# Attention and mixture of experts: the causal mask moves from TensorE products to GpSimd selects

## The chip, the cores and the metric

The kernel runs on one core of one Trainium2 chip. The metric is the device time of one execution in microseconds (us). The engines are named as in the profile: PE (TensorE, matrix products), PEld (its weight loads), ACT (ScalarE), DVE (VectorE), POOL or Pool (GpSimd) and SP (SyncE, which issues most DMAs).

## The reference

For x of 8 batch rows x 1024 positions x 512 features (f32), the reference computes

```python
x = x + attn(layernorm(x))      # 16 heads of 32 features
x = x + moe(layernorm(x))       # 8 experts, the best 2 per token, capacity 160 per batch row
```

In the attention, Q and K of a head are the cosines and sines (from an interpolated table) of angles that depend on x and on the position, 64 features each; V is the sum of such a cosine and sine. What matters here:

```python
scores = jnp.einsum('bqhd,bkhd->bhqk', Q, K) / scale
causal = jnp.triu(jnp.ones((S, S), dtype=bool), k=1)
scores = jnp.where(causal, -jnp.inf, scores)
attn = jax.nn.softmax(scores, axis=-1)
```

The experts' part picks two experts per token, gives each token a slot of its expert (at most 160 per batch row and expert; the rest is dropped), runs two matrix layers with relu, and adds the gated rows back.

## The kernel before

**Steps.** The attention runs in 32 steps `n`; step n works on batch row b = n // 4 and a group c = n % 4 of four heads, which are two pairs of heads. For each pair, and for each half h of the queries (512 of 1024), `scores` makes tiles of scores with the keys on the 128 partitions and the queries along the row, for both heads of the pair at once: 128 x 2 x 512 in two PSUM banks. A half h has 4h full tiles with earlier keys and then four blocks of keys of its own half, which are cut by the diagonal: the first block has 512 queries, the second 384, the third 256, the fourth 128. `tiles_of` puts the second and the fourth into one tile, so a half has 4h + 3 tiles, and three of them need the mask, with four diagonal blocks of 128 x 128 in all.

**Scores, weights, sums.** The products of K and Q (line L679) use 64 rows of PE each, so the two heads of a pair run side by side. ACT takes the exponential of a tile from PSUM to a tile `e` in SBUF (L699); it subtracts no maximum. `attend` then multiplies `e` with V (L713); a column of V that holds a constant makes the sum of the weights, by which `turn` divides later (transposes L215 into PSUM, reciprocal L748, product L750).

**The mask before.** Behind the score products of a tile with own keys, PE adds a large negative number to the scores of later keys: `keys_b` (rows of an identity, bf16) times `later_b` (0 or -FAR, bf16), in two parts of 64 keys for each of the two heads, that is four small products per tile (L693). The exponential makes zeros of these. `rest_of_loads` and `mask` prepare `keys_b` and `later_b` on Pool at the start.

**The order of the work.** PE, ACT, DVE and SP run in the order in which the program is written (`manual_schedule`); Pool's order is a planner's, except where `keep_in_program_order` holds an instruction in the written order. The written order interleaves generators: `some(5, *ahead)` makes the next five score tiles, `some(3, *products)` the next three tiles of `attend`. A plain step has four bursts of score tiles:

1. all three tiles of the first pair's half 0 and two of its half 1; then the last four tiles of the previous step's last `attend`,
2. the other five tiles of half 1; then `turn` of the previous step, and all of `attend` for the first pair (3 + 7 tiles),
3. for the second pair two tiles of half 0, `turn` of the first pair, the third tile, two tiles of half 1; in three of four steps the transposes for the step after next; then `attend` for half 0 (3 tiles),
4. the other five tiles of half 1; then, in the next step, `attend` for half 1.

The score tiles, the transposes of `turn`, those of Q and K and the router's products share three PSUM buffers of two banks (`two_banks`).

**Angles.** For the next steps DVE makes the angles of Q and K from transposed x (L520, into `qk_f`), shifts them (L440, `angle`, into `qk_r`), ACT squares (L444, `square`), takes absolute values (L580) and sines (L589, L447), and DVE multiplies (L450, `times`) into `qk_c` and `qk_r`; SP's DMAs carry these into the layout of the score products (L604). `qk_r` and `qk_c` have one buffer each. V's angles go through L621, L626 and L440, the output's through L642, L440, L450 and L653. ACT loads a table between sines and exponentials, twice a step.

**Router and scatters.** In the steps of batch row b the router of row b - 1 runs in pieces (`router`; layer norm L807, products L869 and L852, choice of experts L876 to L968). It ends in step c = 3 with a list `scatters` of 16 entries, one for each 128 tokens and choice: an indirect DMA on Pool that writes token numbers and gates to the experts' slots in DRAM (L764). Each waits for the landing of the one before, since they write one tensor. `scatter()` issues all 16 at that place, for rows 0 to 5; for the last two rows they are issued in `ending`, half of row 6's first. `fetch_slots` (L991) brings the finished slots of a row into SBUF two batch rows later in the program; the planner places it.

**The experts** follow the attention (L1175 and L1220, a Strassen-like scheme). Weight mixtures of the first of them run on Pool (L1159), in written order.

The parts of `scores` that the change touches, in the program's own words:

```python
own_keys = parts[0][0] >= 4 * h
...
        nc.tensor.matmul(
            out_, lhsT=keys_b[r, part, :], rhs=late,
            start=False, stop=part == 1, skip_group_check=True,
        )
e = ep.tile([P, 2, n], F32, name=f"e_{n}", bufs=8 if n == 512 else 2)
```

Of the kernel before, what the change touches and what calls it, by code (L numbers as in the profile page):

```python
# [11 lines left out]
F32 = mybir.dt.float32  # L12
I32 = mybir.dt.int32
U16 = mybir.dt.uint16
BF16 = mybir.dt.bfloat16
AF = mybir.ActivationFunctionType
ALU = mybir.AluOpType
# [4 lines left out]
P = 128  # L22
B, S, D = 8, 1024, 512
H, DH = 16, 32
NT = B * S
NTT = S // P
NCH = D // P
# [28 lines left out]
UNIT = COS_HALF / LIFT  # L56
# [7 lines left out]

FIRST = 6 * P
REACH = [(0, -(-FIRST // CAP)), (FIRST // CAP, B)]

FAR = 1000.0 * math.sqrt(2 * DH) / (UNIT * UNIT)

ROOT_GUESS = float(0x5F3759DF)  # L70

# [2 lines left out]
def preln_attn_moe_kernel(  # L74
# [21 lines left out]
    nc = tc.nc  # L96
# [35 lines left out]
    own = to_router.pool("own", 1, **left)  # L132
# [3 lines left out]
    row2 = to_router.pool("row2", 2, **left)  # L136
# [44 lines left out]
    ident = const.tile([P, P], F32, name="ident")  # L181
# [4 lines left out]
    for t in (base_first, room[0]):  # L186
        nc.gpsimd.iota(
            t, pattern=[[0, 2], [1, S]], base=0, channel_multiplier=0,
# [19 lines left out]
    def two_banks():  # L208
        return ps_sc.tile([P, 2, 512], F32, name="ps_s")
# [21 lines left out]
    def first_stats(t0, t1):  # L231
        for t in range(t0, t1):
            st = small.tile([P, nc.vector.BN_STATS_DIM], F32, name="st")
            nc.vector.bn_stats(st, first_tiles[t])
            nc.vector.bn_aggr(first_mv[:, t, :], st)
# [14 lines left out]
    ps = two_banks()[:, 0, : 6 * NCH]  # L250
# [8 lines left out]
    nc.gpsimd.memset(ones, 1.0)  # L259

    before = own.tile([P, P], F32, name="before")


    keys_b = own.tile([P, 2, P], BF16, name="keys_b")
    nc.gpsimd.memset(keys_b, 0.0)
    later_b = own.tile([P, 2, P], BF16, name="later_b")
    e_row = own.tile([P, E], F32, name="e_row")
    e_row_low = own.tile([P, E], F32, name="e_row_low")
    dropped = own.tile([P, NTT, TOPK], F32, name="dropped")
# [12 lines left out]
    empty = own.tile([P, E * CAP // P, 2], I32, name="empty")  # L282
    nc.vector.memset(empty, 0)

    later = row2.tile([P, NCH, 2 * P], F32, name="xT", bufs=1)[:, :3, :P]

    def mask():
        for part in range(2):
            for a in range(2):
                r = slice(a * 64, (a + 1) * 64)  # L290
                nc.gpsimd.tensor_copy(later_b[r, part, :], later[r, 1 + part - a, :])
                nc.gpsimd.tensor_copy(keys_b[r, part, part * 64 : part * 64 + 64], ident[r, r])

    def rest_of_loads():

        nc.gpsimd.memset(later, 0.0)
        for i in range(3):
            nc.gpsimd.affine_select(
                out=later[:, i, :], in_=later[:, i, :], compare_op=ALU.is_ge, fill=-FAR,
                base=64 * (1 - i), pattern=[[1, P]], channel_multiplier=-1,  # L300
            )
        nc.gpsimd.affine_select(
            out=before, in_=ones, compare_op=ALU.is_gt, fill=0.0, base=0, pattern=[[1, P]],
            channel_multiplier=-1,
        )
        nc.gpsimd.iota(
            e_row, pattern=[[1, E]], base=0, channel_multiplier=0,
            allow_small_or_imprecise_dtypes=True,
        )
        nc.gpsimd.iota(  # L310
            e_row_low, pattern=[[1, E]], base=-E, channel_multiplier=0,
            allow_small_or_imprecise_dtypes=True,
        )
        nc.gpsimd.iota(
            dropped, pattern=[[P * TOPK, NTT], [1, TOPK]], base=E * CAP,
            channel_multiplier=TOPK, allow_small_or_imprecise_dtypes=True,
        )
        nc.gpsimd.iota(
            empty[:, :, 0], pattern=[[0, E * CAP // P]], base=NT, channel_multiplier=1
        )  # L320
        for a in range(2):
            nc.sync.dma_start(
                inv_o[a * 64 : a * 64 + DH, :],
                w_out.rearrange("(q a d) -> a d q", a=2, d=DH)[a],
            )
        nc.sync.dma_start(wr_sb[:, :, :E], Wr.rearrange("(c p) e -> p c e", p=P))
        nc.vector.tensor_reduce(
            gather_e, ident.rearrange("p (c k) -> p k c", k=32)[:, :E, :], AX.X, ALU.add
        )
        nc.sync.dma_start(br_b, br.partition_broadcast(P))  # L330
        for i in range(NCH):
            nc.sync.dma_start(out[NT:, i * P : (i + 1) * P], zero)
            for t in xn2_d:
                nc.sync.dma_start(t[t.shape[0] - P :, i * P : (i + 1) * P], zero)
        for b in range(B):
            nc.sync.dma_start(
                slot_d[b][: E * CAP, :].rearrange("(p j) c -> p (j c)", p=P),
                empty.rearrange("p j c -> p (j c)"),
            )
# [319 lines left out]
    def tiles_of(h):  # L659


        def block(kb, at=0):
            q0 = max(512 * h, kb * P)
            return kb, q0, 512 * (h + 1) - q0, at

        d = 4 * h
        full = [[block(kb)] for kb in range(d + 1)]
        return full + [[block(d + 1), block(d + 3, 3 * P)], [block(d + 2)]]

    def scores(pair, h, es):  # L670

        for parts in tiles_of(h):
            n = sum(w for _, _, w, _ in parts)
            ps = two_banks()
            own_keys = parts[0][0] >= 4 * h
            for kb, q0, w, at in parts:
                for a in range(2):
                    r = slice(a * 64, (a + 1) * 64)
                    nc.tensor.matmul(  # L679
                        ps[:, a, at : at + w], lhsT=pair[r, 1, kb * P : (kb + 1) * P],  # L680
                        rhs=pair[r, 0, q0 : q0 + w], start=at == 0, stop=not own_keys,
                        skip_group_check=True,
                    )
            if own_keys:

                for part, w in ((0, 64), (1, P)):
                    for a in range(2):
                        r = slice(a * 64, (a + 1) * 64)
                        out_, late = ps[:, a, :w], later_b[r, part, :w]
                        if len(parts) == 2:  # L690
                            out_ = ps[:, a, :].rearrange("p (k q) -> p k q", q=P)[:, ::3, :w]
                            late = late.unsqueeze(1).to_broadcast([64, 2, w])
                        nc.tensor.matmul(  # L693
                            out_, lhsT=keys_b[r, part, :], rhs=late,
                            start=False, stop=part == 1, skip_group_check=True,
                        )

            e = ep.tile([P, 2, n], F32, name=f"e_{n}", bufs=8 if n == 512 else 2)
            nc.scalar.activation(  # L699
                e, ps[:, :, :n], AF.Exp, scale=UNIT * UNIT / math.sqrt(2 * DH)  # L700
            )
            es.append(e)
            yield

# [48 lines left out]
        )  # L753


    scatters = []
    scattered = {b: [] for b in range(B)}
    mixed = []

    def scatter(count=2 * NTT * TOPK, together=False):  # L760

        for _ in range(min(count, len(scatters))):
            b, idx, src = scatters.pop(0)
            queued = nc.gpsimd.indirect_dma_start(  # L764
                out=slot_d[b], out_offset=bass.IndirectOffsetOnAxis(ap=idx, axis=0),
                in_=src, in_offset=None,
            )
            ins = queued.ins
            if together:
                tc.add_manual_dep(  # L770
                    ins, mixed[-1].name,
                    mybir.DependencyInfo(
                        mybir.DependencyClass.NoSync, mybir.DependencyReason.DATA
                    ),
                    reason="behind the mixture",
                )
                for other in scattered[b]:
                    tc.declare_no_dep(ins, other, reason="rows of their own")
            scattered[b].append(ins)

    def router(b):
# [556 lines left out]
    next(base0)  # L1338
    next(base1)
    rest_of_loads()  # L1340
    mask()
    first_stats(2, NTT)
    layernorm_first()
    rest(base0)
# [12 lines left out]
    for n in range(NCK):  # L1357
        more, late = n + 1 < NCK, last is not None
        b, c = divmod(n, NCH)
# [87 lines left out]
        if c == 3 and b > 0:  # L1447
            next(route)
            if b > 1:
                fetch_slots(b - 2)  # L1450
            if b < B - 1:
                scatter()


        some(3, *products)
# [61 lines left out]
    def ending():  # L1517

        o_st = o_pre(NCK - 1, pos_n)
        scatter(NTT * TOPK // 2, together=True)  # L1520
        yield
        sine(o_st[1])
        square(o_st[0])
        for _ in range(3):
            yield
        for _ in o_post(NCK - 1, o_st):
            yield
        yield
        for name in router(B - 1):
            if name == "tiles":  # L1530
                scatter(together=True)

            for _ in range({"tiles": 5, "places": 5}.get(name, 1)):
                yield
        fetch_slots(B - 2)
        scatter(together=True)
        fetch_slots(B - 1)
# [33 lines left out]
```

## Time and profile before

| what | value |
|---|---|
| time, median of 3 runs | 3274.41 us (3272.74 to 3276.23) |
| time of the profiled execution | 3277.64 us |
| its span, first to last instruction | 3275.9 us |
| mean granted clock of PE | 0.996 |
| busy PE / DVE / ACT / POOL, share of the span | 97% / 69% / 40% / 13% |
| mask products L693 | 1536, first at 36.4 us, last at 1274.1 us |
| exponentials L699 | 640, mean 938 ns |
| scatters L764 | 128, mean 1268 ns |

Times in the views are microseconds from the first instruction unless marked ns. A line of a timeline gives start, duration, engine, line of the kernel, operation, output and inputs by the program's names, shapes, and the number of instructions merged; in brackets the idle time of the engine just before, and what ended it. A line of the waits gives who waited for whom, the sum in us, how many times, and the longest. A line of the stretches gives a window, its length, and the busy time and number of instructions of each engine. Ends of matmuls are modelled by the profiler, so starts are the safer figures.

### The profile page before, as it was taken

What the parts mean: (1) busy time and instruction counts of PE and PEld (TensorE: products, weight loads), DVE (VectorE), ACT (ScalarE), POOL (GpSimd) and SP (SyncE); (2) the same over time, 40 slices, a digit from 0 to 9 for tenths busy, and PEclk for the clock granted to TensorE, in tenths of its full rate; (3) what the DMA queues carried; (4) which work ended last, traced back from release to release, by engine and by line L of the source; (5) the groups of instructions that cost most, each with busy time, mean ns of one, the idle gap of its engine ahead of it and who ended that gap; (6) DMA issues with size and microseconds to landing.
All of it is one profiled execution on the core that took longest, in us unless ns stands there. A gap on an engine that the chain in (4) does not pass through costs nothing.

```text
span 3275.9 us, 48751 instructions
## 1 busy us (share of the span) xinstructions
PE 3190.8 (97%) x18942; PEld 2164.6 (66%) x18942; DVE 2255.8 (69%) x4961; ACT 1323.3 (40%) x1617; POOL 426.2 (13%) x387
## 2 busy tenths in 40 slices
PE   5999999999999999999999999999999999999998
PEld 2444444444444444588688688688688688688687
DVE  8887888878788675755755855855855855855854
ACT  7888887878787874201201201201201201201201
POOL 3000202011110213311011011011011011011010
PEclk9999999999999999999999999999999999999999
DMA  5435454453645352322322322322322322322321
GB/s 162 143 97 166 133 147 139 132 155 104 181 114 158 91 162 70 114 54 73 103 46 73 103 46 73 103 47 72 103 48 71 104 48 69 106 49 69 105 42 26
DMA packets 235254, 319.74 MB, mean 98 GB/s; under 512 B 22456, under 2 KB 155280, under 8 KB 222992
## 3 DMA queue, kind: packets, MB, share of 16 engines
q1 hardware_dynamic: 211664, 273.38, 28.6%
q0 software_dynamic: 22912, 43.22, 7.4%
q8 instruction: 150, 2.46, 0.3%
q14 instruction: 80, 0.66, 0.1%
q10 hardware_dynamic: 448, 0.02, 0.0%
HBM read 187.62 MB, written 61.82 MB: 76 GB/s over the span
## 4 chain that ended last, share of the span: by engine, by line
PE 57%; DVE 0%; DMA 0%; issue 0%; POOLq 0%; POOL 0%; DVEq 0%
PE ps_p L1220 29%; PE ps_p L1175 27%; PE ps_t L1121 1%; DMA slots<-slot_d 0%; DMA out_dram<-y,slots 0%; DVE w L1053 0%; DVE w_t L1054 0%; DVE w_t L1052 0%; DVE w_t L1055 0%; POOLq L1567 0%; POOL slot_d L764 0%; POOL slots L991 0%; DVE y L1236 0%; DVE p L1257 0%; DVE p L1258 0%
## 5 line engine op out<-in xcount | busy, mean ns | idle before, releaser
L699 ACT ACTIVATE e<-ps_s 128x1024 f32<-128x1024 f32 (+1 forms) x640 | 569.7, 938 | 202.5 <-PE ps_s L679 113.6
L679 PE MATMUL ps_s<-qk 64*128 64x512 f32 (+3 forms) x3072 | 601.9, 507 | 40.3 <-DMA qk<-qk_r 12.4
L1220 PE MATMUL ps_p<-w,hid 128*128 128x256 f32 x2560 | 567.1, 379 | 0.0
L1220 PEld LDWEIGHTS ps_p<-w,hid 128*128 128x128 f32 x2560 | 484.0, 190 | 66.6 <-DVE hid L1193 0.5
L713 PE MATMUL av<-e,v 128*64 128x512 f32 (+3 forms) x3072 | 524.7, 491 | 0.0
L1220 PE MATMUL ps_p<-w_t,hid 128*128 128x256 f32 x1920 | 430.5, 379 | 2.0 <-DVE w_t L1054 2.0
L679 PEld LDWEIGHTS ps_s<-qk 64*128 64x128 f32 x3072 | 262.0, 188 | 231.4 <-issue 111.7
L1220 PEld LDWEIGHTS ps_p<-w_t,hid 128*128 128x128 f32 x1920 | 361.1, 190 | 50.1 <-DVE w_t L1054 2.8
L713 PEld LDWEIGHTS av<-e,v 128*64 128x64 f32 x3072 | 200.8, 137 | 284.7 <-issue 268.1
L1175 PE MATMUL ps_p<-xe,w 128*128 128x256 f32 (+1 forms) x1024 | 297.8, 434 | 0.0
L1175 PE MATMUL ps_p<-xe_s,t 128*128 128x256 f32 (+1 forms) x1024 | 296.9, 433 | 0.0
L1175 PE MATMUL ps_p<-xe,t 128*128 128x256 f32 (+1 forms) x1024 | 296.8, 433 | 0.0
L764 POOL DMA_INDIRECT slot_d<-token,slot x128 | 162.4, 1268 | 974.3 <-issue 627.4
L1251 ACT COPY p<-ps_p 128x256 f32<-128x256 f32 x40 | 14.7, 369 | 604.3 <-PE ps_p L1220 604.3
L1175 PEld LDWEIGHTS ps_p<-xe,t 128*128 128x128 f32 x1024 | 194.4, 190 | 80.9 <-issue 0.4
L1175 PEld LDWEIGHTS ps_p<-xe_s,t 128*128 128x128 f32 x1024 | 194.3, 190 | 80.7 <-issue 0.4
L1175 PEld LDWEIGHTS ps_p<-xe,w 128*128 128x128 f32 x1024 | 193.4, 190 | 80.8 <-DVE hid L1193 3.5
L1080 POOL DMA_INDIRECT xg<-xn_d,source x76 | 75.2, 990 | 1074.8 <-PE ps_t L1121 1064.0
L1242 POOL DMA_INDIRECT out_dram<-y,slots x80 | 126.5, 1582 | 624.1 <-DVE y L1237 624.1
L1190 ACT ACTIVATE p<-ps_p,b_t 128x256 f32<-128x256 f32 (+1 forms) x128 | 65.5, 511 | 336.2 <-PE ps_p L1175 182.1
L1207 ACT ACTIVATE hid<-hid,b_more 128x256 f32<-128x256 f32 (+1 forms) x128 | 71.8, 561 | 274.8 <-DVE hid L1206 270.0
L1194 ACT ACTIVATE hid<-hid 128x256 f32<-128x256 f32 (+1 forms) x128 | 60.1, 470 | 299.5 <-DVE hid L1193 295.3
(224 smaller groups left out, 3818.6 us busy)
## 6 DMA issues: line engine op xcount, KB each, us to landing
w<-in_L_ffn_W_dram SPq DMA_DIRECT2D x256, 256.0 KB
w<-in_L_ffn_W_dram SPq DMA_DIRECT2D x64, 512.0 KB
qk<-qk_c SPq DMA_DIRECT2D x124, 256.0 KB
qk<-qk_r SPq DMA_DIRECT2D x124, 256.0 KB
qk_base<-base_d SPq DMA_DIRECT2D x28, 1024.0 KB
xn_d<-xn SPq DMA_DIRECT2D x72, 256.0 KB
x_mid<-in_L_attn_x_dram SPq DMA_DIRECT2D x16, 1024.0 KB
out_dram<-x_mid SPq DMA_DIRECT2D x8, 2048.0 KB
```

Of the source, the lines that this page charges most:

```text
L679: nc.tensor.matmul(ps[:, a, at : at + w], lhsT=pair[r, 1, kb * P : (kb + 1) * P], rhs=pair[r, 0, q0 : q0 + w], start=at == 0, stop=not own ...
L699: nc.scalar.activation(e, ps[:, :, :n], AF.Exp, scale=UNIT * UNIT / math.sqrt(2 * DH))
L713: nc.tensor.matmul(av[a * 64 : (a + 1) * 64, q0 - 512 * h :], lhsT=vt[:, kb, 2 * pr + a, :], rhs=es[i][:, a, at : at + w], start=kb == 0, ...
L764: queued = nc.gpsimd.indirect_dma_start(out=slot_d[b], out_offset=bass.IndirectOffsetOnAxis(ap=idx, axis=0), in_=src, in_offset=None,)
L1080: ins = nc.gpsimd.indirect_dma_start(out=xg, out_offset=None, in_=xn2_d[i % 2], in_offset=bass.IndirectOffsetOnAxis(ap=source[:, e, j0 + j ...
L1121: nc.tensor.transpose(ps[:, c, :], xg[:, c * P : (c + 1) * P], ident)
L1175: nc.tensor.matmul(ps, lhsT=weights[:, k, :], rhs=rows[:, k, :], start=k == 0, stop=k == 1)
L1190: nc.scalar.activation(p1, product(b11, a11), AF.Identity, bias=b1_t[:, e * NHC + q : e * NHC + q + 1])
L1194: nc.scalar.activation(h11, h11, AF.Relu)
L1207: nc.scalar.activation(h12, h12, AF.Relu, bias=more)
L1220: nc.tensor.matmul(ps, lhsT=hs[k][:, part, cols], rhs=ws[k][weight], start=k == 0, stop=k == NHQ - 1,)
L1242: ins = nc.gpsimd.indirect_dma_start(out=out, out_offset=bass.IndirectOffsetOnAxis(ap=meta[:, e, jj[r], 0:1], axis=0), in_=ys[r], in_offse ...
```

## The change

The bf16 products and what they are made from are gone. Instead, behind the exponential of a tile with own keys, Pool sets the weights of later keys to zero in place, one instruction for each diagonal block (128 keys x 2 heads x 128 queries). These instructions keep the written order. Scatters are issued two at a time behind the last tile of each half's scores, also in written order, rather than all 16 at one place; `hold` keeps row 6's back for `ending`, as before.

```diff
-FAR = 1000.0 * math.sqrt(2 * DH) / (UNIT * UNIT)
...
-    keys_b = own.tile([P, 2, P], BF16, name="keys_b")
-    nc.gpsimd.memset(keys_b, 0.0)
-    later_b = own.tile([P, 2, P], BF16, name="later_b")
...
-    later = row2.tile([P, NCH, 2 * P], F32, name="xT", bufs=1)[:, :3, :P]
-
-    def mask():
...
-        nc.gpsimd.memset(later, 0.0)
-        for i in range(3):
-            nc.gpsimd.affine_select(
...
     def scores(pair, h, es):
-        for parts in tiles_of(h):
+        tiles = tiles_of(h)
+        for parts in tiles:
...
-                        rhs=pair[r, 0, q0 : q0 + w], start=at == 0, stop=not own_keys,
+                        rhs=pair[r, 0, q0 : q0 + w], start=at == 0, stop=True,
...
-            if own_keys:
-
-                for part, w in ((0, 64), (1, P)):
-                    for a in range(2):
-                        r = slice(a * 64, (a + 1) * 64)
-                        out_, late = ps[:, a, :w], later_b[r, part, :w]
-                        if len(parts) == 2:
...
-                        nc.tensor.matmul(
-                            out_, lhsT=keys_b[r, part, :], rhs=late,
-                            start=False, stop=part == 1, skip_group_check=True,
-                        )
 
             e = ep.tile([P, 2, n], F32, name=f"e_{n}", bufs=8 if n == 512 else 2)
             nc.scalar.activation(
                 e, ps[:, :, :n], AF.Exp, scale=UNIT * UNIT / math.sqrt(2 * DH)
             )
+            if own_keys:
+
+                for _, _, _, at in parts:
+                    own_ = e[:, :, at : at + P]
+                    tc.keep_in_program_order(
+                        nc.gpsimd.affine_select(
+                            out=own_, in_=own_, compare_op=ALU.is_ge, fill=0.0, base=0,
+                            pattern=[[0, 2], [1, P]], channel_multiplier=-1,
+                        )
+                    )
+            if parts is tiles[-1] and not hold[0]:
+
+                scatter(2)
             es.append(e)
...
-    scatters = []
+    scatters, hold = [], [False]
...
     def scatter(count=2 * NTT * TOPK, together=False):
...
+            else:
+                tc.keep_in_program_order(queued)
...
     rest_of_loads()
-    mask()
...
-            if b < B - 1:
-                scatter()
+            hold[0] = b == B - 1
```

More of the change, by code (lines that the diff above doesn't have):

```diff
@@ L283, in preln_attn_moe_kernel @@
     nc.vector.memset(empty, 0)
-    later = row2.tile([P, NCH, 2 * P], F32, name="xT", bufs=1)[:, :3, :P]
-    def mask():
-        for part in range(2):
-            for a in range(2):
-                r = slice(a * 64, (a + 1) * 64)
-                nc.gpsimd.tensor_copy(later_b[r, part, :], later[r, 1 + part - a, :])
-                nc.gpsimd.tensor_copy(keys_b[r, part, part * 64 : part * 64 + 64], ident[r, r])
-    def rest_of_loads():
-        nc.gpsimd.memset(later, 0.0)
-        for i in range(3):
-            nc.gpsimd.affine_select(
-                out=later[:, i, :], in_=later[:, i, :], compare_op=ALU.is_ge, fill=-FAR,
-                base=64 * (1 - i), pattern=[[1, P]], channel_multiplier=-1,
-            )
+    def rest_of_loads():
         nc.gpsimd.affine_select(
@@ L680, in scores @@
                         ps[:, a, at : at + w], lhsT=pair[r, 1, kb * P : (kb + 1) * P],
-                        rhs=pair[r, 0, q0 : q0 + w], start=at == 0, stop=not own_keys,
+                        rhs=pair[r, 0, q0 : q0 + w], start=at == 0, stop=True,
                         skip_group_check=True,
                     )
-            if own_keys:
-                for part, w in ((0, 64), (1, P)):
-                    for a in range(2):
-                        r = slice(a * 64, (a + 1) * 64)
-                        out_, late = ps[:, a, :w], later_b[r, part, :w]
-                        if len(parts) == 2:
-                            out_ = ps[:, a, :].rearrange("p (k q) -> p k q", q=P)[:, ::3, :w]
-                            late = late.unsqueeze(1).to_broadcast([64, 2, w])
-                        nc.tensor.matmul(
-                            out_, lhsT=keys_b[r, part, :], rhs=late,
-                            start=False, stop=part == 1, skip_group_check=True,
-                        )
             e = ep.tile([P, 2, n], F32, name=f"e_{n}", bufs=8 if n == 512 else 2)
```

## The prediction

> **What bounds the kernel.** I read the stretches first, then the waits, then the timelines of one step. The attention stage runs to about 1275 us in 32 steps (one batch row and one group of four heads each). Busy time of three successive steps:
>
> ```profile
> core 0: us, PE busy (x) PEld busy (x) DVE busy (x) ACT busy (x) POOL busy (x), PEclk, DMA share, GB/s
> ...
> 845.00:884.00 39.00, 35.74 (x372) 18.66 (x366) 26.06 (x40) 28.36 (x28) 3.67 (x5) 0.96 0.77 230
> 884.00:922.60 38.60, 38.55 (x330) 18.57 (x326) 31.39 (x70) 33.72 (x36) 0.00 (x0) 1.00 0.51 147
> 922.60:961.00 38.40, 38.35 (x314) 19.18 (x314) 32.45 (x68) 34.00 (x35) 5.93 (x4) 1.00 0.51 142
> ```
>
> PE is busy all through a plain step, but ACT (34.0 of 38.4) and DVE (32.5) have only 4.4 and 5.9 us to spare. The first row holds a router's work, and there PE itself has 3.3 us of idle time. After 1290 us PE works on the experts without a gap; the change leaves that part alone. The waits of 60 to 1230 us show a second loop:
>
> ```profile
> DVE qk_r L440 <- DMA qk<-qk_r: 45.9, 23, 3.3
> ...
> ACT qk_f L444 <- DVE qk_r L440: 9.9, 16, 1.6
> ...
> PE ps_s L679 <- DVE prob L876: 9.0, 11, 2.2
> ```
>
> DVE's rotation (L440) waits for the landing of the previous rotation's DMA in 23 steps, ACT's squares (L444) wait for L440 in 16, and the next exponentials come behind the squares on ACT. Once a batch PE waits for the router's DVE chain.
>
> **What is removed.** One score burst on PE:
>
> ```profile
> 923.62 0.25 PE L693 MATMUL ps_s<-later_b,keys_b 64*128 64x64 bf16 x4
> 923.71 1.09 PE L679 MATMUL ps_s<-qk 64*128 64x384 f32 x8
> 924.63 0.33 PE L693 MATMUL ps_s<-later_b,keys_b 64*128 64x128 bf16 x4
> 924.79 0.60 PE L679 MATMUL ps_s<-qk 64*128 64x256 f32 x4
> 925.23 0.25 PE L693 MATMUL ps_s<-later_b,keys_b 64*128 64x64 bf16 x4
> 925.31 1.95 PE L679 MATMUL ps_s<-qk 64*128 64x512 f32 x8
> ```
>
> Matmul ends are modelled, so I take start to start: 0.09 + 0.16 + 0.08 = 0.33 us for twelve mask products. There are 1536, so 128 such sets: 42 us of PE, 1.33 per step. That is the ceiling of the gain.
>
> Not all of it arrives. The step has four bursts of five score tiles, and three PSUM buffers. In the first, ACT runs the five exponentials without a gap (923.97, 4.47 us), and the fifth tile (starting near 926.23) needs the buffer of the second exponential (ending near 926.08): PE comes earlier, but keeps only about 0.1 us. In the second burst the transposes (934.73) need the third exponential (end near 934.45): about 0.2 more is kept. In the third, ACT comes from a table load:
>
> ```profile
> 943.01 1.28 ACT L699 ACT_TABLE_LOAD   x1
> 944.47 2.75 ACT L699 ACTIVATE e<-ps_s 128x1024 f32<-128x1024 f32 x3 [0.17 <-PE ps_s L693]
> ```
>
> It is free at 944.29 and waited 0.17 us for a mask: again 0.15. Only the fourth burst, where ACT waits 2.50 us for PE, keeps the whole 0.33. So PE's own loop gives 0.1 + 0.2 + 0.15 + 0.33 = 0.78 us per step. The second loop gives less: exponentials of burst one, transposes of burst two, scores and transposes of burst three, L450 on qk_r (946.95 to 949.23), its DMA, L440 at 956.75 (after 2.3 us of waiting for the landing), squares, next exponentials at 960.10. Masks ahead of its PE parts were worth about 0.2 in burst two and 0.09 + 0.16 in burst three: 0.45 us per step. The slower loop decides; with the 0.1 to 0.3 us that it still has in hand, 0.5. In the seven steps with a router DVE works from 829.4 to 844.6 us with hardly a gap, and PE stands 2.2 us for L876 at 855.4: I give these nothing. Gain: 25 x 0.5 = 12.5 us (bounds 0 and 42).
>
> The mask's preparation (memsets, three affine selects, eight casts, under 4 us on Pool before 17.4 us) goes too. Pool then idles 13.7 us until L566 at 31.4, waiting for DVE: worth nothing. Were that cover gone, 4 us.
>
> **What is added.** Per set four affine selects in place (one, two, one), 512 in all, 128 partitions x 256 elements. Nearest row: L298, 128x128, 284 ns, starts 0.25 apart. A memset grows from 195 ns (128 columns) to 410 (384), so I take 0.4 us (0.25 to 0.5): 205 us of Pool, or 6.4 us per step, beside 162 us of scatters. Pool has room.
>
> Who waits for a select? The second matmul (L713) now waits for Pool where it waited for ACT. In the step shown, burst one's masked exponentials end by 926.6 and are used at 935.3; burst two's end by 936.0 and are used near 941; burst four's by 957.1, used after the next step's burst one. Burst three is the tight one: ended at 945.5, 946.6 and 947.2, used from 949.04: 3.5 us. In a batch's first step no transposes lie between (822.7 to 830.1), the cover is about 3.1 us, and L450 at 827.19 (2.28 us, two SBUF inputs) can hold the last select up: 0.2 us in 8 steps, 1.6 in all (0 to 8).
>
> The large unknown is DVE beside Pool. Pool's scatters wait for such DVE work (one at 940.72 takes 3.00 us instead of 0.96: L450 ran from 940.52 to 942.80), and DVE's median times beside scatters do not change. But beside Pool arithmetic that reads SBUF they do:
>
> ```profile
> 1331.23 0.72 POOL L1159 TENSOR_TENSOR t<-w,t 128x256 f32<-128x256 f32 x1
> 1331.91 0.73 POOL L1159 TENSOR_TENSOR t<-w 128x256 f32<-128x256 f32 x1
> ```
>
> ```profile
> 1331.26 0.22 DVE L927 TENSOR_REDUCE gate<-prob 128x8 f32<-128x64 f32 x1
> 1331.52 0.51 DVE L928 TENSOR_TENSOR tmp<-prob,gate 128x64 f32<-128x64 f32 x1
> 1332.07 0.65 DVE L929 SCALAR_TENSOR_TENSOR tmp<-tmp,e_row 128x64 f32<-128x64 f32 x1
> 1332.75 0.22 DVE L930 TENSOR_REDUCE exp_id<-tmp 128x8 f32<-128x64 f32 x1
> ```
>
> L928 and L929 take 0.23 us alone; the reductions, with one input, keep their 0.22. With L920 (0.72) and L932 (0.40) four instructions lose 1.36 us beside four Pool instructions of 0.73: 47% of Pool's time. L807, a one-input form, goes from 0.54 to 1.03 beside the same line at 1317.7. A 0.4 us select would so cost 0.19 us where DVE does nothing but such forms. Forms with two SBUF inputs (L450, L621, L626, L642, L653), and with one like L807 (L440, L414), are about 15 of the 38.4 us of a step, 40%: 0.075. A select held by one of them starts exactly at its end, in front of the next, so I take 0.1 us (0 to 0.19): 1.6 us of DVE per step.
>
> The Trainium skill, "SBUF — State Buffer", section "Who interferes with whom", speaks against this change: of VectorE (with two SBUF inputs or in a two-port mode) and GpSimd, whichever starts first holds the shared ports for its whole instruction, and the other stands. By that rule a collision can cost a whole select: at most 0.4 x 40% x 16 = 2.6 us of a router step and 0.8 of another, and the sum below would end at about +27 us rather than +10.
>
> Where it lands: in the seven router steps DVE is the bound, 7 x 1.6 = 11 us. In the other 25 most of it goes into DVE's idle 5.9 us. But L450 on qk_r follows 0.4 us after the end of an exponential whose two selects come then, and L440 (956.75) lies just behind the one that ends at 956.49: half a select each, 0.4 us per step on the second loop, 10 us (0 to 20).
>
> **Scatters.** Sixteen per batch remain, now in pairs at the end of each half's scores, in queue with the selects. The second of a pair waits for the landing of the first (236.4 us over 89 waits, at most 6.3), and the next selects stand behind it. Between burst two's last select (near 936.5) and burst three's first use (949.0) there are 12.4 us; a pair takes 0.96 + 2.7 + 0.96 typically: nothing. The two fetches of slots (L991) behind the last pair add a landing of at most 6.2 and 1.6 us, once a batch: 0 (0 to 10 in all). In the first step the position rows of L463 waited on Pool until 51.22 for a DMA; selects queued behind that would hold PE about 6 us, once: 0 (0 to 6). At the end the second weight mixture (1236 before) now comes after the last select (1275) but is used after 1290: nothing; the eight scatters behind it follow and still end before the next mixture at 1289.
>
> **Sum.** -12.5 + 1.6 + 11 + 10 = +10 us on the profiled execution's 3277.6 (span 3275.9). The median of three runs is 3.2 us below that, 3274.4; moved by 10 it is 3284.
>
> **Rivals.** *Collisions are rare* (faster): if a select costs DVE 0.02 us or less, the loops run at their gain, 25 x 0.5 to 32 x 0.78: -12 to -25 us, about 3254. For it: DVE has 5.9 idle us per step; nothing shows an affine select beside DVE. It decides below about 0.05 us per select. *Pool's queue* (slower): a pair with both waits at their longest takes 3.0 + 6.3 + 3.0 = 12.3 us, as much as the 12.4 us of cover; with the fetches behind it, 6 us late once a batch: 3274 + 36, less a few, about 3300. Against it: typical waits are 2.7 us. *A wash*: 0.5 gained, 0.5 lost per step, 3274.
>
> **Chances.** Collisions on DVE, the forecast: 0.41, 3284 (+7 to +35). Pool's queue: 0.12. Wash: 0.17. Rare collisions: 0.30. Slower by over 0.2% (6.5 us, about what these runs can tell): 0.53; within: 0.17; faster: 0.30. The range is 3252 to 3316: below, the middle of the third case; above, both slow cases with DVE's loss near its bound.
>
> **What would show it.** Right: L693 gone; selects near 0.4 us; L621, L626, L414 and L440 longer in the mean; DVE busier by 1 us or more per step; L444 waiting longer for L440; PE with idle time in front of L679. Wrong: DVE's means unchanged and steps near 37.8 us; or L713 waiting for Pool.

## The result, and the profile after

The changed kernel takes 3284.8 us (median of 8 runs, 3282.4 to 3288.0) where the kernel before took 3276.2 beside it (8 runs, 3272.7 to 3277.5): a ratio of 1.0030 (95% interval 1.0021 to 1.0039), some 9 us slower. The profiled execution has a span of 3282.9 us; before it was 3275.9. The forecast, 3284, is hit within a microsecond; the working below it is not, as the runs show.

The lines keep their meaning with new numbers: scores L658 (L679 before), exponentials L665 (L699), products of weights and V L692 (L713), rotation L418 (L440), squares L422 (L444), products on `qk_r` L428 (L450), scatters L743 (L764), router L857 (L876). The selects are L673. First the three stretches that the prediction showed, with windows at the same distance from DVE's work on `qk_r` (columns: window, its length, busy time of each engine with its number of instructions, granted clock, DMA):

```profile
core 0: us, PE busy (x) PEld busy (x) DVE busy (x) ACT busy (x) POOL busy (x), PEclk, DMA share, GB/s
853.62:894.81 41.19, 36.06 (x339) 17.83 (x340) 28.79 (x43) 28.31 (x28) 13.37 (x18) 0.96 0.70 214
894.81:933.91 39.10, 37.65 (x284) 17.34 (x283) 32.15 (x70) 33.49 (x37) 11.23 (x19) 1.00 0.51 151
933.91:972.63 38.72, 37.38 (x254) 17.11 (x252) 33.35 (x68) 33.38 (x35) 12.52 (x20) 1.00 0.50 139
```

A plain step has 0.90 to 0.97 us less of PE work (38.55 and 38.35 before) and is still 0.3 to 0.5 us longer; PE, which had 0.05 us of idle time in it, now has 1.3 to 1.5. DVE gained 0.8 to 0.9 us. The step with the router's work (first row) is 2.2 us longer, 41.19 for 39.00. Who PE waits for stands in the waits between 60 and 1230 us (sum, times, longest):

```profile
ACT L665 <- PE ps_s L658: 53.6, 30, 2.9
PE ps_s L658 <- ACT e L665: 46.0, 69, 3.3
...
DVE qk_r L418 <- DMA qk<-qk_r: 23.1, 21, 3.3
...
PE ps_s L658 <- DVE prob L857: 7.3, 8, 2.6
...
PE av L692 <- POOL e L673: 4.7, 7, 0.7
...
ACT qk_f L422 <- DVE qk_r L418: 3.7, 11, 0.7
```

PE waited for ACT's exponentials for 4.0 us before and 46.0 now. The second loop has become easier: the rotation waits 23.1 us for its landing (45.9 before), the squares 3.7 for the rotation (9.9). So what holds PE is not the loop that the forecast named. The first line has no counterpart before, and no output name: it is ACT's table load. The timeline of burst three, in the step that the prediction showed:

```profile
955.69 1.46 PE L658 MATMUL ps_s<-qk 64*128 64x512 f32 x10
...
956.40 1.28 ACT L665 ACT_TABLE_LOAD   x1 [1.42 <-PE ps_s L658]
...
957.70 2.48 ACT L665 ACTIVATE e<-ps_s 128x1024 f32<-128x1024 f32 x3
...
958.58 2.28 DVE L428 SCALAR_TENSOR_TENSOR qk_r<-qk_f,qk_r 128x2048 f32<-128x2048 f32 x1
...
958.77 0.70 PE L658 MATMUL ps_s<-qk 64*128 64x256 f32 x4 [1.13 <-ACT e L665]
958.79 3.06 POOL L673 TENSOR_SCALAR_AFFINE_SELECT e<-e 128x256 f32<-128x256 f32 x3 [10.11 <-ACT e L665]
```

Before, ACT loaded the exponential's table as soon as its sines were done (943.01), and was ready when the first score tile came. Now it stands idle for 1.42 us until that tile is there, and then loads for 1.28 us with the tile waiting; PE finds its three buffers full and waits 1.13 us. The reason stands in the program. An exponential has to wait for two engines now, for PE (its scores) and for Pool (the select that last wrote the reused tile `e`). The wait for PE has become an instruction of its own, and in all 32 steps it stands ahead of the table load:

```
before: LoadActFuncSet
        Activation e<-ps_s [waits PE]
after:  EventSemaphore [waits PE]
        LoadActFuncSet
        Activation e<-ps_s [waits Pool]
```

The selects themselves, over the whole execution (busy, mean of one):

```profile
L673 POOL TENSOR_SCALAR_AFFINE_SELECT e<-e 128x256 f32<-128x256 f32 x512 | 311.8, 635 | 625.2 <-ACT e L665 624.2
L743 POOL DMA_INDIRECT slot_d<-token,slot x128 | 151.9, 1186 | 168.2 <-DMA slot_d<-token,slot 138.5 <-issue 15.6 <-DVE token L949 14.1
```

One undisturbed takes 0.41 us; the mean of 0.635 comes of selects held by DVE, as at 958.79, where three take 3.06 us: the first is held until L428 is done at 960.86, and the other two follow.

### The profile page after: what moved, and what is told of

Its sections match the earlier page's. It is cut to its first block, busy times and chain, and to the rows that moved or that the text cites. A ratio compares the mean times of both kernels' runs of the same rounds, so it can differ in the third digit from the quotient of the medians.

```text
span 3282.9 us, 46266 instructions
## 1 busy us (share of the span) xinstructions
PE 3155.2 (96%) x17406; PEld 2115.6 (64%) x17406; DVE 2275.3 (69%) x4961; ACT 1308.0 (40%) x1617; POOL 721.4 (22%) x886
## 4 chain that ended last, share of the span: by engine, by line
PE 57%; DVE 0%; DMA 0%; issue 0%; POOLq 0%; POOL 0%; DVEq 0%
PE ps_p L1201 29%; PE ps_p L1156 27%; PE ps_t L1102 1%; DMA out_dram<-y,slots 0%; DMA slots<-slot_d 0%; DVE w_t L1035 0%; DVE w L1034 0%; DVE w_t L1033 0%; POOLq L1546 0%; DVE w_t L1036 0%; POOL slot_d L743 0%; POOL slots L972 0%; DVE y L1217 0%; DVE p L1238 0%; DVE p L1239 0%
## 5 line engine op out<-in xcount | busy, mean ns | idle before, releaser
L658 PE MATMUL ps_s<-qk 64*128 64x512 f32 (+3 forms) x3072 | 569.6, 504 | 77.4 <-ACT e L665 48.7
L665 ACT ACTIVATE e<-ps_s 128x1024 f32<-128x1024 f32 (+1 forms) x640 | 556.0, 943 | 176.1 <-PE ps_s L658 173.2
L692 PE MATMUL av<-e,v 128*64 128x512 f32 (+3 forms) x3072 | 527.7, 492 | 9.2 <-POOL e L673 9.2
L658 PEld LDWEIGHTS ps_s<-qk 64*128 64x128 f32 x3072 | 263.1, 188 | 350.7 <-issue 150.0
L673 POOL TENSOR_SCALAR_AFFINE_SELECT e<-e 128x256 f32<-128x256 f32 x512 | 311.8, 635 | 625.2 <-ACT e L665 624.2
L692 PEld LDWEIGHTS av<-e,v 128*64 128x64 f32 x3072 | 200.6, 137 | 304.5 <-issue 256.7
L743 POOL DMA_INDIRECT slot_d<-token,slot x128 | 151.9, 1186 | 168.2 <-DMA slot_d<-token,slot 138.5
```

The source lines that it names most:

```text
L658: nc.tensor.matmul(ps[:, a, at : at + w], lhsT=pair[r, 1, kb * P : (kb + 1) * P], rhs=pair[r, 0, q0 : q0 + w], start=at == 0, stop=True, s ...
L665: nc.scalar.activation(e, ps[:, :, :n], AF.Exp, scale=UNIT * UNIT / math.sqrt(2 * DH))
L673: nc.gpsimd.affine_select(out=own_, in_=own_, compare_op=ALU.is_ge, fill=0.0, base=0, pattern=[[0, 2], [1, P]], channel_multiplier=-1,)
L692: nc.tensor.matmul(av[a * 64 : (a + 1) * 64, q0 - 512 * h :], lhsT=vt[:, kb, 2 * pr + a, :], rhs=es[i][:, a, at : at + w], start=kb == 0, ...
L743: queued = nc.gpsimd.indirect_dma_start(out=slot_d[b], out_offset=bass.IndirectOffsetOnAxis(ap=idx, axis=0), in_=src, in_offset=None,)
```

## The experiments

The theory from the trace: **the late table load** holds PE, 32 times 1.3 us. (From the last of `turn`'s transposes to burst three's next scores, start to start, PE takes 1.35 us in each of the 32 steps, where it took 0.06: 41.5 us more in all, of which the profile books 36 as idle time.) Its rivals are the prediction's theory, **DVE's collisions**, and **Pool's queue**. All times are compared as ratios to the kernel before on the same chip; 0.001 is 3.3 us.

**1. The load made early, in the changed kernel.** Behind the last sine of each step:

```diff
         if late:
             sine(o_st[1])
+        nc.scalar.activation(warm, split_c, AF.Exp)
```

> The changed kernel with one more one-column exponential on ACT, on data that are long there, right behind the turn's last sine of each step, so that the exponential's table is loaded before burst three's first score tile is ready. Table-load theory: the changed kernel's trace shows the load (1.28 us) behind the first score tile in all 32 steps and 41 us of PE idle behind it; taken away, the kernel comes 25 to 41 us below the changed kernel's 3284.8, at 3244 to 3260, and so faster than the kernel before. Prediction's theory (DVE slowed by the selects holds the loops): the load's 1.3 us per step lies beside the second loop's wait, and the time stays within 5 us of the changed kernel's. Pool's-queue theory: no change either, within 5 us.

Measured: 3254.4 us, ratio 0.9955 (0.9941 to 0.9968): 25 us below the changed kernel, 15 below the kernel before. Its timeline:

```profile
929.79 1.28 ACT L1441 ACT_TABLE_LOAD   x1
...
931.08 0.20 ACT L1441 ACTIVATE warm<-split_c 128x1 f32<-128x1 f32 x1
931.21 2.48 ACT L665 ACTIVATE e<-ps_s 128x1024 f32<-128x1024 f32 x3
...
932.29 0.70 PE L658 MATMUL ps_s<-qk 64*128 64x256 f32 x4
```

The load runs while PE still makes the tile, and PE goes on without a gap at 932.29. Both rivals had said "within 5 us". Of the 41.5 us 25 came. That the second loop is next to bind fits the rest, since its waits grew (23.1 and 3.7 us in the changed kernel):

```profile
DVE qk_r L418 <- DMA qk<-qk_r: 60.7, 23, 4.9
ACT qk_f L422 <- DVE qk_r L418: 26.6, 29, 2.3
...
PE ps_s L658 <- ACT e L665: 22.6, 51, 4.3
```

**2. The same line in the kernel before**, as a control.

> Control: the same early one-column exponential in the kernel before, where the trace shows the table load already ahead of the first score tile. Table-load theory: within 4 us of the kernel before, since nothing waited for the load there (4.9 us of waits at most). Prediction's theory: the same, within 4 us; were it faster by more than 10, the dummy would do something else than moving the load.

Measured: 1.0000 (0.9991 to 1.0009). Where the load was already early, the dummy changes nothing.

**3. The load made late in the kernel before**, masks still as products, by a one-column sine of burst three's first tile ahead of its exponential:

```diff
+            if first:
+                nc.scalar.activation(warm, ps[:, 0, :1], AF.Sin, scale=0.0)
             nc.scalar.activation(
                 e, ps[:, :, :n], AF.Exp, scale=UNIT * UNIT / math.sqrt(2 * DH)
             )
```

> The kernel before with a one-column sine of burst three's first score tile put ahead of its first exponential, so that the load of the exponential's table comes behind that tile, as in the changed kernel. Masks stay products, no selects. Table-load theory: 32 x 1.28 us of load and some 0.2 us for the sine itself, of which most reaches the end: 30 to 47 us slower than before, 3305 to 3322. Prediction's theory (the second loop has only a little in hand and PE's loop the rest; burst three's load lies in a stretch in which ACT waits anyway): at most 10 us slower.

Measured: 1.0109 (1.0094 to 1.0125), 36 us. With no select anywhere, the load behind the tile costs what the theory said (30 to 47 us, with some 0.2 us a step for the sine itself):

```profile
964.63 0.17 ACT L700 ACTIVATE warm<-ps_s 128x1 f32<-128x1 f32 x1 [1.47 <-PE ps_s L694]
964.81 1.28 ACT L702 ACT_TABLE_LOAD   x1
966.10 2.50 ACT L702 ACTIVATE e<-ps_s 128x1024 f32<-128x1024 f32 x3
```

**4. The mask products taken out, with nothing in their place.** This kernel, and those built on it in 5 and 8, leave the causal mask out.

```diff
-                        rhs=pair[r, 0, q0 : q0 + w], start=at == 0, stop=not own_keys,
+                        rhs=pair[r, 0, q0 : q0 + w], start=at == 0, stop=True,
...
-            if own_keys:
-                for part, w in ((0, 64), (1, P)):
...
-                        nc.tensor.matmul(
-                            out_, lhsT=keys_b[r, part, :], rhs=late,
```

> The kernel before without its twelve mask products per set, and with nothing in their place: it leaves out the causal mask. It measures the gain alone. Prediction's own term: 12.5 us less (3262), bounds 0 and 25. Table-load theory, which takes the 42 us of removed PE work as nearly all on the path: 30 to 42 us less (3232 to 3244).

Measured: 0.9890 (0.9875 to 0.9905), 36 us of the 42 us that the products take. The prediction's 12.5 is a third of it.

**5. Idle selects.** On a scratch tile, behind each masked tile's exponential, whose end releases them; nothing waits for them:

```diff
+            if own_keys:
+                for _ in parts:
+                    sel = nc.gpsimd.affine_select(
+                        out=idle_w, in_=idle_w, compare_op=ALU.is_ge, fill=0.0, base=0,
+                        pattern=[[0, 2], [1, P]], channel_multiplier=-1,
+                    )
+                    tc.keep_in_program_order(sel)
+                    tc.add_manual_dep(
+                        sel.ins, exp_.ins.name,
...
```

Added to the kernel of 4:

> The kernel before without its mask products (the causal mask is left out) and with the 512 selects on a scratch tile, each released by the end of its tile's exponential; no exponential and no product of weights and values waits for Pool, the scatters stand as before. The early-load kernel lies 20 us above the one without masks (3254.4 and 3234.2). Collision theory (selects slow DVE through SBUF, and the second loop with it): most of the 20 us comes back, 3246 to 3258. Data-wait theory (second products and reused tiles wait for Pool's queue): the time stays within 5 us of 3234.

Measured: 0.9926 (0.9913 to 0.9940), 12 us above the kernel of 4 (by the two intervals 5 to 18). Its selects are held as those of the changed kernel are, 659 ns in the mean:

```profile
L692 POOL TENSOR_SCALAR_AFFINE_SELECT idle_w<-idle_w 128x256 f32<-128x256 f32 x497 | 327.3, 659 | 458.9 <-ACT e L687 435.7
```

But the exponential's table comes early again, with no dummy. The rows of its load, with ACT's idle time ahead of it last, of the kernel before, the changed kernel and this one:

```profile
L699 ACT ACT_TABLE_LOAD x33 | 42.3, 1283 | 5.4 <-PE ps_s L693 4.9
```

```profile
L665 ACT ACT_TABLE_LOAD x33 | 42.3, 1283 | 60.8 <-PE ps_s L658 60.8
```

```profile
L687 ACT ACT_TABLE_LOAD x33 | 42.3, 1283 | 4.7 <-PE ps_s L681 4.1
```

So it is not Pool's being busy that makes the load late, but that the exponential waits for Pool.

Added to the kernel before, products kept:

> The kernel before, masks still as products, with the same 512 idle selects beside it. Prediction's collision term alone: 11 us in the router steps and 10 us on the second loop, 21 us above the kernel before. Table-load theory with collisions as a smaller part: 5 to 20 us above it, and the table load still unhindered; if the selects cost nothing here, within 4 us.

Measured: 1.0013 (1.0004 to 1.0022), 4 us. So the selects, by their presence alone, cost 4 us where PE has its old work to cover them, and 12 where it has not: real, and about half of what the prediction gave collisions.

**6. The scatters at one place again**, sixteen in a row as before, in the changed kernel and in that of 1.

```diff
-            if parts is tiles[-1] and not hold[0]:
-                scatter(2)
...
-            else:
-                tc.keep_in_program_order(queued)
...
-            hold[0] = b == B - 1
+            if b < B - 1:
+                scatter()
```

> The changed kernel with its scatters where the kernel before has them, sixteen in one place. Pool's-queue theory (selects late behind pairs of scatters): 20 us or more faster than the changed kernel; or, with sixteen in a row ahead of selects, slower by more than 20. Table-load and collision theories: within 6 us of the changed kernel.

> The changed kernel with the early exponential (3254.4) and with sixteen scatters in one place. Pool's-queue theory: with the load hidden, the queue shows, and the time differs from 3254 by 10 us or more. Collision theory: within 6 us of 3254.

Measured: 1.0792 (1.0777 to 1.0807) and 1.0698 (1.0683 to 1.0713), some 245 us above their counterparts' 1.0030 and 0.9955. It is the second way in which the Pool's-queue theory could go:

```profile
PE av L689 <- POOL e L673: 196.9, 11, 39.6
```

```profile
765.26 0.97 POOL L740 DMA_INDIRECT slot_d<-token,slot  x1 [1.89 <-DMA slot_d<-token,slot]
767.63 0.97 POOL L740 DMA_INDIRECT slot_d<-token,slot  x1 [1.41 <-DMA slot_d<-token,slot]
768.62 1.48 POOL L673 TENSOR_SCALAR_AFFINE_SELECT e<-e 128x256 f32<-128x256 f32 x4
```

```profile
769.08 3.13 PE L689 MATMUL av<-e,v 128*64 128x512 f32 x8 [39.62 <-POOL e L673]
```

The first is the waits of the kernel with sixteen, the second its timeline on Pool, the third on PE: each scatter waits for the landing of the one before, the selects stand behind all sixteen, and PE for the selects, here for 39.6 us; the trace has six such places, 231 us in all. (The granted clock is 0.56 from 730 to 768 us, while PE stands, and 0.75 from 769 to 775, when it works again; then it is 1.00.) Scattering in pairs is therefore a part that the selects need, not an extra.

**7. One scatter at a time** in the kernel of 1.

```diff
-                scatter(2)
+                scatter(1)
```

> The changed kernel with the early exponential and with its sixteen scatters one at a time behind each of a batch's sixteen score bursts, instead of two at a time behind eight of them. 9 us lie between the early-load kernel (0.9955 of the kernel before) and the one with idle selects (0.9926). If selects held by the second scatter of a pair make them (5.3 us of PE idle before the second products were put down to Pool), 4 to 9 us below the early-load kernel, 0.993 to 0.994; if collisions of the dependent selects with DVE make them, within 3 us of it.

Measured: 0.9962 (0.9948 to 0.9976), the same as with pairs. Pool waits less for landings, and nothing comes of it; the first line is with pairs, the second with single ones:

```profile
POOL slot_d L743 <- DMA slot_d<-token,slot: 151.5, 60, 6.4
```

```profile
POOL slot_d L743 <- DMA slot_d<-token,slot: 7.2, 6, 1.5
```

**8. Where the 9 us between 0.9926 and 0.9955 lie.** The kernel of 4 with idle selects, and now with the scatters in pairs too.

```diff
+            if parts is tiles[-1] and not hold[0]:
+                scatter(2)
...
+            else:
+                tc.keep_in_program_order(queued)
...
-            if b < B - 1:
-                scatter()
+            hold[0] = b == B - 1
```

> The kernel with idle selects and no products (the causal mask is left out; 0.9926 of the kernel before), with its scatters in pairs behind the score bursts, in one order with the selects, as the changed kernel has them. Nothing waits for a select. If the 9 us up to the early-load kernel (0.9955) come from where the scatters now stand, it goes up by 6 to 10 us, to 0.9945 to 0.9957. If they come from products and exponentials that wait for the selects' results, it stays within 3 us, 0.992 to 0.9935.

Measured: 0.9969 (0.9959 to 0.9979), 14 us above the same kernel with the scatters issued as before. With nothing waiting for a select, the whole distance is there: it is the scatters' new order and what moves with it, not the products that wait for Pool. The rotation's wait for its landing, 41.8 us with the old order, is here

```profile
DVE qk_r L442 <- DMA qk<-qk_r: 50.6, 21, 4.9
```

Among the plain steps the growth sits in one of each batch row, the one behind the router's. There the stretch from the end of DVE's product on `qk_r` to the rotation behind its transfer takes 10.4 us for 8.5 (mean of six), and the step is 0.9 us longer; in the other plain steps the stretch stays as it was (6.84 for 6.85 and 7.17 for 7.15). The first batch row's such step, which has nothing to fetch yet, did not grow either (8.34 for 8.44). No scatter is issued in that step, in either kernel. What has come there are the row's two fetches of slots, which wait for the last scatter: they are issued from 7 us before to 2 us behind the end of the product and take 5.8 to 8.2 us to land, where with the old order they came 16 us or more away from it and landed in 2.5 to 4.3. Scatters beside the transfer go with a longer stretch too: in run 7, five stretches that had none with pairs and have one with single scatters went from 6.85 to 7.7 us. No run moved the fetches alone, and the six steps make some 6 of the 14 us; where the rest comes from stays open.

**9. Products kept in some bursts**, selects in the others, with the early load: in burst three alone, then in bursts one and three. The second pair's line is shown; `products` is false for the first pair in the first of the two kernels.

```diff
-        ahead = [scores(pairs[1], h, es[h]) for h in range(2)]
+        ahead = [scores(pairs[1], h, es[h], h == 0) for h in range(2)]
...
-            if own_keys:
+            if own_keys and products:
...
+            if own_keys and not products:
```

> The early-load kernel with products instead of selects in burst three alone, the burst whose selects start with DVE's rotation on qk_r (2.38 us in the mean there, 2.28 in the kernel before). It gives back 0.33 us of PE work per step there, of which 0.15 to 0.33 reach the end: 5 to 10 us. If burst three's selects are what keeps the second loop late, the gain is 5 to 12 us and the sum between -7 and +5 us, 3247 to 3260 on the scale of the early-load kernel's 3254; if their part is small, 5 to 10 us slower than it.

> The same with products in bursts one and three, so that selects stand only behind bursts two and four. In burst one ACT sets the pace, so that the prediction's working has 0.23 us of the 0.33 hidden there: at most 3 us more on PE than with burst three alone, less what the eight selects per step that go cost on DVE (by the 12 us of the idle selects, some 6). Expected: from 6 us below to 3 us above the version with products in burst three alone. If every removed product counts in full, as the 35 of 42 us without masks suggest, 8 to 10 us above it.

Measured: 0.9984 (0.9975 to 0.9994) and 0.9987 (0.9978 to 0.9996). Products in burst three cost 9 us more than selects there (by the two intervals 4 to 15), about their 32 x 0.33 us; those in burst one cost 1 more, less than the noise. Neither comes near the kernels of 1 and 7, the fastest of all that compute the mask.

## Why the prediction was right, and where its working was wrong

The sum has the right value, but from terms of which most have the wrong size. From the ratios, at 3.27 us for 0.001; the runs' column adds up by construction, since each entry is the difference of two kernels that stand next to each other:

| step of the prediction | predicted, us | the runs, us | from |
|---|---|---|---|
| products removed | -12.5 (0 to -42) | -36 | 0.9890 |
| selects beside DVE's work | 11 + 10 = +21 | +12 | 0.9926 - 0.9890 |
| scatters in pairs, and the fetches behind them | 0 (0 to 10) | +14 | 0.9969 - 0.9926 |
| waiting for the selects | +1.6 (0 to 8) | none seen (-5) | 0.9955 - 0.9969 |
| table load in burst three | not late | +25 | 1.0030 - 0.9955 |
| sum | +10 | +10 | 1.0030 |

Each difference is uncertain by 5 to 7 us; the runs come from several chips, each beside its own runs of the kernel before. That the sum agrees is luck: the gain was put 23.5 us too small, collisions 9 us and waiting for the selects some 7 us too large, and 14 us of scatters and 25 of the table load were put at nothing; these errors cancel.

**The gain** failed at "the slower loop decides": the prediction took 0.45 us per step for the second loop because masks of some bursts lie outside it, and gave router steps nothing. Between one product on `qk_r` and the next (mean of six batches) the step without products is shorter by 0.8, 1.0 and 1.4 us in the three shorter steps of a batch row, and by 2.0 in the longest, which holds most of the router (40.9 for 42.8). The rotation's wait stays (43.0 us, 45.9 before): both loops got shorter together, since the second one runs through PE's bursts one, two and three. Its 0.1 to 0.3 us "in hand" were read from a wait, not from how it moves.

**The table load** is the step that decided the sign. The prediction read the row of the load, saw it hidden, and wrote "again 0.15" for burst three. It asked who waits for a select and answered with the products L713; it did not ask for the other user, the exponential that overwrites the tile eight tiles later. That wait is never long in itself, and no row of the profile before could show where the program would put it. Its price could have been bounded from the row shown: 32 x 1.28 = 41 us.

**Collisions on DVE** were the named mechanism, and only part of what happened. DVE's busy time grew from 2255.8 to 2275.3 us, 0.6 us per step where 1.6 were forecast. In the router step a little over half of it came: idle selects make it 0.9 us longer, the full change with the load early 1.0 (41.8 for 40.9). In two of the others idle selects cost at most 0.04 us, where 0.4 had been given, and 0.2 in the third. Undisturbed and disturbed rows of the changed kernel show why: L428 on 128x2048, the longest, keeps its 2.28 us, and the selects are what stands; L620 goes from 1.23 to 1.36 and L418 on 128x1024 from 0.69 to 0.78 in the median beside Pool.

The Trainium skill, "SBUF — State Buffer", section "Who interferes with whom", says that the engine that comes first holds the shared ports for its whole instruction and the other stands. For Pool the rows agree: the first select at 958.79 comes 0.21 us behind L428 and ends at 961.13, behind L428's end at 960.86. For DVE they fall short of it: in the kernel of 1 a select begins at 933.22, L428 at 933.38, and L428 takes 2.39 us for 2.28, a loss of 0.11 where the select had some 0.25 to go.

**Scatters**: "a pair takes 0.96 + 2.7 + 0.96 typically: nothing" is right for Pool's queue, as run 7 shows, and the 12.4 us of cover nearly held (PE waits 4.7 us for selects between 60 and 1230 us). The term asked only whether selects come late behind the scatters and the fetches. It missed that their new place costs 14 us with nothing waiting for a select; of these, some 6 lie in the step where the fetches stand beside the transfer of `qk_r`.

**Rivals.** *Pool's queue* is out for the changed kernel (the same 4.7 us) and would have been the case by far had the scatters stayed where they were. *Rare collisions* forecast 12 to 25 us less than before, and the kernel with the early load has 15 less, but for other reasons: 12 us of collisions and 14 of scatters against a gain of 36. *A wash* was out by the interval.

Of the signs that the text listed, PE's idle time in front of the scores came (L658, 40.3 us before and 77.4 after, over the whole execution), but nearly all of the growth is the 36 us behind the late load and tells nothing of collisions. DVE got busier, by 0.6 us per step where 1 was asked for. L444 waiting longer for L440 did not come (9.9, now 3.7): the sign that told the forecast mechanism from the real one.

## What to carry to other kernels

When an edit gives an instruction a second engine to wait for, look at what stands directly ahead of it in its queue: a table load that ran in idle time can be made to wait in its place, and then PE waits for the load too: here 1.30 us each time, 41.5 us in all, of which 25 reached the end. A tiny instruction of the same function, with nothing to wait for, put where the engine idles, brings the load back; here it turned 0.3% slower into 0.45% faster. And price a removed piece of work on every loop that passes through its engine, since a loop that looks like the limit may be shortened by the same edit.

## What the runs showed of the hardware

The Trainium skill, "ScalarE: Activation LUTs", section "What ACT_TABLE_LOAD costs", gives a switch some 1283 ns of loading and 1380 ns of drain, 2.66 us in all. The loading is what these rows show. The drain is not to be seen: the exponential follows 0.02 us behind the load (956.40 + 1.28, then 957.70), ACT is idle for 0.2 us in all ahead of the 32 loads of experiment 1, which come straight behind a sine, and the 32 late loads cost 41.5 us of PE's time. An estimate from the page's figure would be 32 x 2.66 = 85.

A DVE instruction of 2.28 us holds a select of 0.41 us that comes behind it as long as it lasts, and loses nothing itself; one that comes behind a select loses about 0.1 us; 512 selects that nothing waits for cost 4 us or 12, by what else the loops have to do.
